# Sorting out graph edges: a threshold on GpSimd for four rows, an edge count in place of tie tests, and one sine for the weights

## The chip, the cores and the metric

The kernel runs on one core of a Trainium2 chip. The metric is the device time of one execution in microseconds (us). The kernel before the change takes 1742.52 us, the median of 4 runs (1740.88 to 1758.24).

## The reference

There are 128 graphs of 64 nodes with 128 features, and a 64x64 matrix of distances for each graph, of which about a quarter is not zero. Four graph layers run one after the other, each as `x = layernorm(x + layer(x, adj))`. The first two are continuous-filter layers, and nearly all work lies in them:

```python
# layer 0 (layer 1 is alike: 64 Gaussians, weight A*A in place of rcut)
f_ij = exp(coeff * (d_ij - offsets)**2)
rcut = 0.5 * (cos(d_ij * pi / 5.0) + 1.0) * (d_ij < 5.0)
y    = x @ w_in2f
W    = (ssp(f_ij @ fw1 + fb1) @ fw2 + fb2) * rcut[..., None]
agg  = einsum('bjf,bijf->bif', y, W)
out  = ssp(agg @ ow1 + ob1) @ ow2 + ob2
```

Layers 2 and 3 are graph convolutions with a normalised adjacency matrix. In layer 0 an edge counts only if its distance is under 5, in layer 1 only if it isn't zero. Since `0.5 (cos(pi d / 5) + 1)` is the square of `sin(pi/2 - pi d / 10)`, the weight of layer 0 can be had from one sine and a square.

## The kernel before

**Slots in place of dense matrices.** The kernel computes filters only for edges that are there. The 64 rows of a graph are put in order of their degree, and eight rows each share a partition group; a row gets as many slots as a fixed table of capacities (CAPS) gives it. For each pair of graphs the slots' distances `d`, column numbers `j` and weights `w` lie in DRAM and are loaded by `loads` two pairs ahead, on the queue of SP. Should the input not fit the assumptions (too many edges in a row, equal distances, and the like), a flag sends the program into a general path at the end; with these inputs it isn't taken.

**The main loop.** Two layers of 64 pairs with three chunks each give 384 iterations. An iteration runs, for a chunk: `filter_in` (TensorE, then Exp and Ln on ScalarE), `gather` (TensorE with a one-hot matrix built on VectorE, then a copy on ScalarE), `filter_out` (TensorE), `message` (VectorE, line 1753, two instructions a chunk), and the sums over slots (VectorE, lines 1777 and 1781). The instructions of TensorE, ScalarE, VectorE, GpSimd and SP stand in the order in which the program issues them (`in_order`), so that each engine works through one fixed queue. Small jobs are Python generators in queues; `run(queue, n)` takes n steps of one. `early` holds the edge search, `side` the spreading of the edges for layer 1, one step an iteration.

**The edge search.** The pairs fall into eight sets of eight (NS = 8). `compact(s)` calls `nearest(s)`, which has the eight rows of a set in a tile `ad` of 128 partitions x 8 rows x 64 columns. It turns distances to negative numbers and absent edges to -1e30 (FAR) and then goes through up to five rounds (ROUNDS): MAX8 finds the eight largest values of a row (into `top`, line 1148), FIND_INDEX8 their columns (`at`, line 1151), and MATCH_REPLACE8 puts -1e30 in their places (line 1155), so that the next round finds the next eight. Tests for equal neighbours and for rows that aren't exhausted follow (lines 1163 to 1172). `pack` copies the found values into dense slots (`dc`, `jc`, on GpSimd except in part of set 0), stores them, and computes the weight `w` with a rounding, an absolute value, a sine on ScalarE, a square, and two masks (lines 1088 to 1098). Set 0 is searched ahead of the loop; sets 1 to 7 are searched inside it, during layer 0. `spread_out` puts between the steps of one set the scatters that prepare the next (`permuted`, `load_x`), one in every PACE steps. The loop takes nine steps of `early` an iteration up to iteration 18, and then PACE on average. After the sets, `late_constants` prepares layers 2 and 3 with further steps.

**Where GpSimd comes in.** Its queue carries the scatters (lines 1008 and 1272, indirect DMAs), the packing copies (1070, 1084), the layernorm's power and scaling (1367, 1372), and the adding of biases (1393, 1624).

## Time and profile before

| | |
|---|---|
| median of 4 runs | 1742.52 us (1740.88 to 1758.24) |
| profiled execution | 1747.6 us, span 1745.8 us, mean granted clock 0.949 |
| PE busy | 1544.4 us (88%), 6812 instructions |
| VectorE (DVE) busy | 1532.6 us (88%), 4485 instructions |
| ScalarE (ACT) busy | 1353.1 us (78%), 1699 instructions |
| GpSimd (POOL) busy | 754.2 us (43%), 1150 instructions |
| MATCH_REPLACE8, line 1155 | 176 instructions, 35.1 us, and as many value loads, 13.8 us |

PE is TensorE's matmuls, PEld its loading of weights, SP the engine that issues most DMAs. The shares are of the whole span; the first 90 us are preparation, layer 0 lasts to about 865 us, and the last 150 us run out with less work. An engine that is 88% busy on average can be full in one stage and wait in another, so the shares must be read by stage.

### The profile page before, as it was taken

To read this page: it belongs to the slowest core of one execution; us is meant where nothing else is said; L and a number is where in the kernel's file an instruction comes from. 1 tells how busy PE (TensorE), PEld (TensorE's weight loads), DVE (VectorE), ACT (ScalarE), POOL (GpSimd) and SP (SyncE) were. 2 spreads that over 40 slices of the span, in tenths; PEclk is the share of its full clock that TensorE was granted. 3 is DMA by queue.
4 is the path that set the end of the run, shared out by engine and by line. 5 is a ranking of instruction groups with operands and counts; after the bars stand their busy time and mean duration, and the time that the engine had idled before them with its cause. 6 is when DMAs were issued, how large, how long until landed. Compare 5 with 4: busy or idle time off the path is not lost.

```text
span 1745.8 us, 24319 instructions
## 1 busy us (share of the span) xinstructions
PE 1544.4 (88%) x6812; PEld 798.0 (46%) x6812; DVE 1532.6 (88%) x4485; ACT 1353.1 (78%) x1699; POOL 754.2 (43%) x1150
## 2 busy tenths in 40 slices
PE   1267799999998989898999999999999999999975
PEld 1123344444444444444544555555555555554444
DVE  6668699999998989889888899999999899998875
ACT  1246678888887878787999988889888888888731
POOL 2354154553646543234411234455443445553434
PEclk9978789999998989899999999999999999999976
DMA  4353354545453544343666655545555454555200
GB/s 148 84 131 93 85 129 115 139 120 132 125 137 94 137 104 121 99 114 94 150 146 147 136 124 119 139 121 140 124 129 128 109 138 114 144 121 134 56 8 21
DMA packets 112658, 202.86 MB, mean 116 GB/s; under 512 B 47214, under 2 KB 63872, under 8 KB 112384
## 3 DMA queue, kind: packets, MB, share of 16 engines
q1 hardware_dynamic: 99856, 185.24, 43.8%
q0 software_dynamic: 8080, 14.47, 2.8%
q10 hardware_dynamic: 4576, 1.49, 0.4%
q8 instruction: 56, 0.92, 0.2%
q14 instruction: 90, 0.74, 0.2%
HBM read 186.66 MB, written 14.45 MB: 115 GB/s over the span
## 4 chain that ended last, share of the span: by engine, by line
PE 34%; DVE 22%; issue 14%; DMA 10%; POOL 10%; ACT 4%; SPq 4%; another core or an unknown queue 1%; ACTq 0%; DVEq 0%; POOLq 0%
PE pw L1725 12%; PE pg L1738 7%; PE px L1712 6%; DMA out_dram<-gz,at_row 6%; DVE m L1753 5%; POOL x_all L1372 3%; DVE agg L1777 3%; SPq L1246 2%; ACT h L936 2%; DVE hot L1697 2%; POOL rs L1367 2%; POOL gz L1372 2%; DVE at L1151 1%; DMA w<-w_dram 1%; PE o L1527 1%
## 5 line engine op out<-in xcount | busy, mean ns | idle before, releaser
L936 ACT ACTIVATE g<-pg 128x672 f32<-128x672 f32 (+12 forms) x384 | 298.9, 778 | 168.4 <-PE pg L1738 124.7
L1738 PE MATMUL pg<-hot,ys 64*128 64x336 f32 (+12 forms) x1536 | 354.8, 540 | 11.8 <-ACT g L936 6.2
L936 ACT ACTIVATE h<-h,half 128x672 f32<-128x672 f32 (+13 forms) x385 | 351.1, 912 | 12.5
L1725 PE MATMUL pw<-h,w_L_gnn_fw 128*128 128x336 f32 (+6 forms) x768 | 287.6, 500 | 48.4 <-DVE m L1753 43.0
L1777 DVE TENSOR_REDUCE agg<-m 128x16 f32<-128x240 f32 (+13 forms) x896 | 325.0, 411 | 2.4
L1725 PE MATMUL pw<-h,w_L_gnn_W2T 128*128 128x420 f32 (+5 forms) x768 | 302.6, 517 | 3.1 <-DVE m L1753 3.0
L1753 DVE SCALAR_TENSOR_TENSOR m<-pw,c_L_gnn_fb,g 128x336 f32<-128x336 f32 (+6 forms) x384 | 202.3, 565 | 41.9 <-PE pw L1725 16.8
L1753 DVE SCALAR_TENSOR_TENSOR m<-pw,c_L_gnn_b,g 128x420 f32<-128x420 f32 (+5 forms) x384 | 225.9, 625 | 10.3 <-PE pw L1725 7.5
L1712 PE MATMUL px<-d,fw 32*128 32x336 f32 (+6 forms) x768 | 171.1, 522 | 49.7 <-ACT d L936 29.7
L936 ACT ACTIVATE h<-px,c_L_gnn_b 128x840 f32<-128x840 f32 (+5 forms) x192 | 176.8, 921 | 45.2 <-PE px L1712 43.3
L1738 PEld LDWEIGHTS pg<-hot,ys 64*128 64x128 f32 x1536 | 119.5, 191 | 197.1 <-ACT h L936 93.5
L1725 PEld LDWEIGHTS pw<-h,w_L_gnn_fw 128*128 128x128 f32 x768 | 140.9, 203 | 148.4 <-DVE m L1753 86.5
L1725 PEld LDWEIGHTS pw<-h,w_L_gnn_W2T 128*128 128x128 f32 x768 | 132.7, 191 | 128.4 <-issue 31.2
L1367 POOL TENSOR_TENSOR rs<-rs,neg_half 128x4 f32<-128x4 f32 x61 | 69.0, 1131 | 274.3 <-DVE rs L1364 272.5
L1697 DVE SCALAR_TENSOR_TENSOR hot<-j,row,w 128x1212 f32<-128x1212 bf16 (+12 forms) x128 | 175.5, 1371 | 11.7 <-DMA w<-w_dram 11.2
L936 ACT ACTIVATE h<-px,c_L_gnn_fb 128x672 f32<-128x672 f32 (+6 forms) x192 | 158.4, 825 | 22.6 <-PE px L1712 9.3
L1712 PE MATMUL px<-d,w1t 64*128 64x420 f32 (+5 forms) x768 | 169.1, 517 | 0.0
L936 ACT ACTIVATE d<-d,neg_off 128x1212 f32<-128x1212 f32 (+12 forms) x128 | 136.3, 1065 | 6.4 <-DMA d<-d_dram 6.4
L1712 PEld LDWEIGHTS px<-d,fw 32*128 32x128 f32 x768 | 60.3, 191 | 147.7 <-issue 66.0
L1008 POOL DMA_INDIRECT rows<-comb,goes x64 | 66.9, 1045 | 131.7 <-DMA rows<-comb,goes 79.7
L1372 POOL TENSOR_SCALAR x_all<-ny,mv,rs 128x128 f32<-128x128 f32 x124 | 110.2, 895 | 3.4
L1008 POOL DMA_INDIRECT out_dram<-gz,at_row x56 | 73.0, 1303 | 53.0 <-DMA out_dram<-gz,at_row 40.0
(255 smaller groups left out, 2282.3 us busy)
## 6 DMA issues: line engine op xcount, KB each, us to landing
d<-d_dram SPq DMA_DIRECT2D x32, 315.0 KB
w<-w_dram SPq DMA_DIRECT2D x32, 315.0 KB
d<-d_dram SPq DMA_DIRECT2D x32, 303.0 KB
w<-w_dram SPq DMA_DIRECT2D x32, 303.0 KB
w<-w_dram SPq DMA_DIRECT2D x32, 252.0 KB
j<-j_dram SPq DMA_DIRECT2D x32, 157.5 KB
j<-j_dram SPq DMA_DIRECT2D x32, 151.5 KB
d<-d_dram SPq DMA_DIRECT2D x16, 300.0 KB
```

What stands on the lines that cost most here:

```text
L936: latest = nc.scalar.activation(out_, in_, func, **kw)
L1008: nc.gpsimd.indirect_dma_start(out=into, out_offset=bass.IndirectOffsetOnAxis(ap=at, axis=0), in_=rows, in_offset=None,)
L1151: nc.vector.max_index(out=at[:, r, cut], in_max=top[:, r, cut], in_values=ad[:, r, 0:A])
L1246: (engine if name == "d" else nc.sync).dma_start(to, dram_ap(slots[layer, name][s], first, [[0, to.shape[0]], [1, n]]))
L1367: nc.gpsimd.tensor_tensor(rstd, rstd, neg_half[:, 0:n], ALU.pow)
L1372: (nc.gpsimd if n == GS else nc.vector).tensor_scalar(dst[:, s, :], y[:, s, :], mv[:, s, 0:1], rstd[:, s : s + 1], ALU.subtract, ALU.mult,)
L1697: nc.vector.scalar_tensor_tensor(hots[n][:, 0:size], j[:, 0:size], near, wt[:, 0:size], ALU.is_equal, ALU.mult)
L1712: nc.tensor.matmul(ps[:, b, 0:n], lhsT=w["w1"][rows, :], rhs=d[rows, col : col + n], start=True, stop=True,)
L1725: nc.tensor.matmul(ps[:, 0 : c["size"]], lhsT=c["w"]["w2"], rhs=c["h"][:, b, :], start=True, stop=True)
L1738: nc.tensor.matmul(ps[:, b, 0:n], lhsT=y[rows, :], rhs=hots[c["n"]][rows, at], start=True, stop=True,)
L1753: nc.vector.scalar_tensor_tensor(messages[n][:, b, at], c["pw"][b][:, 0:size], c["w"]["b2"], c["g"][:, b, :], ALU.add, ALU.mult,)
L1777: nc.vector.tensor_reduce(av[:, :, :, r], both, AX.X, ALU.add)
```

## The change

`take_out`, on GpSimd, replaces MATCH_REPLACE8 for sets 1 to 7: for up to four rows at once it subtracts the smallest of the eight values found from each value, turns "not below" into -1e30, and adds that, writing into a second tile, so that rounds alternate between two tiles. Set 0 keeps MATCH_REPLACE8. The tests for ties become a count: the edges found, with a large penalty for each equal pair, are summed into `found`, and `settle` compares the total with the number of edges counted from the input. In `pack` of layer 0 the copy into `dc` becomes a maximum with -5, so that a missing or far edge lies at the distance where the weight is zero, and the weight is one sine and one square, the square on GpSimd for sets 1 to 7. PACE becomes 3, and the uneven 2, 5, 5 steps of an iteration become an even 3.

```diff
-    PACE = 4
+    PACE = 3
...
-            (nc.vector if layer + s == 0 and r % 2 else nc.gpsimd).tensor_copy(
-                dc[:, to], d[:, r, 0 : caps[r]]
-            )
-            if layer == 0 or r % 2:
+            engine = nc.vector if layer + s == 0 and r % 2 else nc.gpsimd
+            if layer == 0:
+                engine.tensor_scalar(dc[:, to], d[:, r, 0 : caps[r]], -CUTOFF, None, ALU.max)
+            else:
+                engine.tensor_copy(dc[:, to], d[:, r, 0 : caps[r]])
+            if r % 2:
                 yield
...
         if layer == 0:
-            nc.vector.tensor_scalar(w, dc, 1.0 / (2 * CUTOFF), MAGIC, ALU.mult, ALU.add)
-            nc.vector.tensor_scalar(w, w, MAGIC, None, ALU.subtract)
-            yield
-            nc.vector.scalar_tensor_tensor(w, dc, 1.0 / (2 * CUTOFF), w, ALU.mult, ALU.subtract)
-            nc.vector.scalar_tensor_tensor(w, w, -1.0, w, ALU.mult, ALU.max)
-            yield
-            act(w, w, AF.Sin, bias=half_pi, scale=-PI)
-            nc.vector.tensor_mul(w, w, w)
-            yield
-            nc.vector.scalar_tensor_tensor(w, dc, -CUTOFF, w, ALU.is_gt, ALU.mult)
-            nc.vector.scalar_tensor_tensor(w, dc, 0.0, w, ALU.is_lt, ALU.mult)
+            act(w, dc, AF.Sin, bias=half_pi, scale=PI / (2 * CUTOFF))
+            yield
+            (nc.gpsimd if s else nc.vector).tensor_tensor(w, w, w, ALU.mult)
...
+        now, then = av, spare_
+
+        def take_out(rows, k):
+
+            least = top[:, rows, 8 * k + 7 : 8 * k + 8].to_broadcast([P, rows.stop - rows.start, A])
+            nc.gpsimd.tensor_tensor(gone[:, rows], now[:, rows], least, ALU.subtract)
+            nc.gpsimd.tensor_scalar(gone[:, rows], gone[:, rows], 0.0, FAR, ALU.is_ge, ALU.mult)
+            nc.gpsimd.tensor_tensor(then[:, rows], now[:, rows], gone[:, rows], ALU.add)
+
         for k in range(max(ROUNDS)):
...
-            for r in now:
-                nc.vector.max(out=top[:, r, cut], in_=ad[:, r, 0:A])
+            for r in range(n):
+                nc.vector.max(out=top[:, r, cut], in_=now[:, r, :])
+                if s > 0 and r + 1 in (4, more) and r < more:
+                    take_out(slice(0 if r < 4 else 4, r + 1), k)
                 yield
...
-        same = big(f"same{s}", 320).rearrange("p (r k) -> p r k", r=8)
-        nc.vector.tensor_tensor(same[:, :, 0:39], top[:, :, 0:39], top[:, :, 1:40], ALU.is_equal)
-        nc.vector.scalar_tensor_tensor(
-            same[:, :, 0:39], top[:, :, 1:40], FAR / 2, same[:, :, 0:39], ALU.is_gt, ALU.mult
...
-        nc.vector.tensor_reduce(odd[:, 5 + s : 6 + s], same[:, :, 0:40], AX.XY, ALU.add)
-        yield
-        nc.vector.scalar_tensor_tensor(top, top, FAR / 2, top, ALU.is_gt, ALU.mult)
-        yield
-        yield from pack(0, s, top, at)
+        yield from pack(0, s, top, at)
...
+        nc.vector.tensor_scalar(edges, top, FAR / 2, None, ALU.is_gt)
+        yield
+        nc.gpsimd.tensor_tensor(equal[:, :, 1:40], top[:, :, 0:39], top[:, :, 1:40], ALU.subtract)
+        nc.gpsimd.memset(equal[:, :, 0], 1.0)
+        nc.gpsimd.tensor_tensor(top, top, edges, ALU.mult)
         nc.gpsimd.tensor_copy(comb[:, :, 1, :], at)
+        yield
+        nc.gpsimd.tensor_scalar(equal, equal, 0.0, -1000.0, ALU.is_equal, ALU.mult)
+        nc.gpsimd.tensor_scalar(equal, equal, 1.0, None, ALU.add)
+        nc.gpsimd.tensor_tensor(equal, equal, edges, ALU.mult)
+        yield from wait_steps(PACE)
+        nc.vector.tensor_reduce(found[:, s : s + 1], equal, AX.XY, ALU.add)
...
-        run(early, 9 if i < 18 else (PACE - 2, PACE + 1, PACE + 1)[k] if i < 3 * (NP - 8) else 7)
+        run(early, 9 if i < 18 else PACE if i < 3 * (NP - 8) else 7)
```

`settle` gains a reduction of `found`, a reduction of the counted degrees, a difference, and a square that is added to the flag.

## The prediction

> **What bounds the kernel now.** I read the shares of the engines first, then the busy time by stage, then the groups of instructions, then the waits. In the busy time by stage the columns are: window, its length, busy time (and instructions) of each engine, granted clock, DMA share, GB/s.
>
> ```profile
> 90.00:190.00 100.00, 66.71 (x223) 28.61 (x223) 67.19 (x292) 51.81 (x65) 47.58 (x62) 0.76 0.42 103
> 250.00:715.00 465.00, 426.63 (x1869) 210.20 (x1868) 435.56 (x1571) 395.15 (x521) 230.91 (x390) 0.95 0.48 123
> 745.00:865.00 120.00, 114.32 (x548) 60.03 (x546) 107.09 (x272) 103.80 (x142) 49.36 (x51) 0.97 0.49 121
> 1100.00:1600.00 500.00, 495.46 (x2322) 266.36 (x2321) 464.96 (x1076) 432.44 (x512) 236.73 (x248) 1.00 0.53 127
> ```
>
> The order is PE, PEld, DVE, ACT, POOL. From 1100 us (second graph layer) PE is busy 99% of the time, and the change touches nothing there. From 250 to 715 us the edges of five sets are found beside the first layer: DVE 94%, PE 92%, POOL 50%. From 745 us the edges are all found: PE 95%, DVE 89%. So the edge search is felt only before about 745 us. The same windows with the message line alone (two instructions a chunk) give the pace:
>
> ```profile
> 250.00:715.00 465.00, 126.81 (x241) 0.95 0.48 123
> 745.00:865.00 120.00, 34.53 (x69) 0.97 0.49 121
> ```
>
> 465 us over 120.5 chunks is 3.86 us a chunk with the search, 120 over 34.5 is 3.48 without it. The later chunks are smaller: a message there takes 34.53/69 = 500 ns against 126.81/241 = 526 ns, so the fair floor is 3.48 x 1.052 = 3.66 us.
>
> **The change on DVE.** The groups of 250 to 715 us, five sets (the last columns are busy us, mean ns | idle before):
>
> ```profile
> L1151 DVE FIND_INDEX8 at<-comb,ad 128x8 uint16<-128x64 f32 x150 | 30.5, 218 | 0.0
> L1148 DVE MAX8 comb<-ad 128x8 f32<-128x64 f32 x150 | 24.4, 213 | 0.6
> L1155 DVE MATCH_REPLACE8 ad<-comb,ad 128x64 f32<-128x64 f32 x110 | 21.9, 209 | 0.0
> L1155 DVE MATCH_VALUE_LOAD ad<-comb,ad 128x8 f32 x110 | 8.7, 79 | 0.0
> ```
>
> Removed per set of eight pairs, for sets 1 to 7: 22 replacements of 209 + 79 ns = 6.34 us; the tie tests (lines 1163 to 1174 without the reduction) 0.47 + 0.48 + 0.47 + 0.48 = 1.90; of the weights (lines 1088 to 1098) six operations, and the square moves to GpSimd: 0.26 + 0.35 + 0.35 + 0.30 + 0.30 + 0.30 + 0.30 = 2.16. Added: one comparison on 128x320, put between nothing and the 0.42 us of line 1141 on 128x512, taken as 0.3. Net 10.1 us a set, 50.5 us for the five. If DVE alone set the pace, 435.6 - 50.5 = 385.1 us at 94% would last 410 us, 55 less. It does not: PE and the floor of 3.66 us come first, and there DVE would stand at 385.1/120.5 = 3.20 us a chunk, 87%, which is the 89% of the stage without search. So 120.5 x (3.86 - 3.66) = 24 us are won, with ends at 17 (PE's own 426.6 us at its later 95.3%, 448 us) and 46 (no correction for size). Chunks from 190 to 250 us run the same mixture: 3 us more. **Steady search: -27 us (-19 to -58, the far end if DVE alone counts).**
>
> The search keeps its place: a set takes 97 steps of the edge queue now (1 + 30 + 30 + 22 + 2 + 12) at four an iteration, and 72 (1 + 30 + 30 + 6 + 2 + 3) at three, 24 iterations both times. The first 18 iterations stay at nine steps, so the search ends some ten iterations earlier and no load of slots comes later.
>
> **The change on GpSimd.** The nearest rows:
>
> ```profile
> L1372 POOL TENSOR_SCALAR x_all<-ny,mv,rs 128x128 f32<-128x128 f32 x124 | 110.2, 895 | 3.4
> L1570 POOL TENSOR_TENSOR blocks<-a_all,dinv 64x256 f32<-64x256 f32 x60 | 37.4, 623 | 79.8 <-DMA out_dram<-gz,at_row 52.5 <-PE nT L1581 18.7 <-PE px L1712 3.5
> L1393 POOL TENSOR_TENSOR x_all<-x_all,b_L_gnn_ob 128x512 f32<-128x512 f32 x16 | 20.6, 1285 | 61.3 <-PE xT L1388 61.3
> L1177 POOL CAST comb<-at 128x320 f32<-128x320 uint16 x8 | 3.6, 447 | 0.0
> ```
>
> Two-input work on 256 elements is 0.62 us. A tensor_scalar with two immediates isn't in the trace: the cast gives 0.36 us for 256 elements as a lower end, line 1372 (0.9 us for 128, two scalars from memory) scaled gives up to 1.8; I take 1.5, since line 1372 is the same operation. take_out for four rows is then 0.62 + 1.5 + 0.62 = 2.7 us (1.6 with the cast; 4.8 if all three run at some 6.2 ns an element like line 1372). A set has five of four rows and two of one row (about 1.0 us): 16 us (10 to 26). After it come two subtracting or masking operations and one more on 320 elements (0.8 each), two tensor_scalars (0.45 to 1.9 each), a memset and the square of w (0.4): 6.5 us, and 1 us because the eight copies into dc become a maximum. In sum 23 us a set (13 to 36) on top of 230.9/5 = 46 us, in 24 x 3.66 = 88 us: POOL goes from 50% to 78% (68 to 93).
>
> The Trainium skill speaks against this: its page "GPSIMD Engine Reference", section "Engine selection", keeps elementwise work on VectorE, with about twice the time for two inputs, and calls one-input work roughly line rate. The trace shows 0.9 us for 128 elements of one-input work at line 1372, so the second half doesn't hold for that form. By the page's line rate my estimate of take_out would be about 1.5 us, and the forecast some 4 us lower.
>
> **New waits.** DVE is one queue in order. MAX8 of the next round waits for take_out; behind it stand messages, slot sums and one-hots, and PE waits for those to free PSUM. take_out is issued after the fourth MAX8, the next round starts 12 steps later: four iterations, 14.6 us. In these POOL has two take_outs (5.5 us), four scatters of the set ahead and four of the spread set with their 0.3 us gaps (10.4), and about 2 us of layernorm: 17.9 us while both run, eight iterations of 24. It falls some 7 us behind and catches up after; with 2.7 us of its own the take_out still lands inside 14.6. Queued before it can also be a scatter that waits for the one before:
>
> ```profile
> POOL dc L1070 <- DVE comb L1174: 69.7, 5, 20.4
> POOL rows L1008 <- DMA rows<-comb,goes: 54.8, 24, 4.2
> ```
>
> That is up to 4.2 us (total, times, longest). So the margin is thin but there. Two places are tighter. The reduction into found comes four to five steps after its POOL chain is issued, about 6 us, and jc's copies, w and the chain need some 8: 2 us of DVE a set. And Sin now waits for POOL's dc instead of a DVE chain: up to 1 us of ACT, with its table load after it; the stores of d, j and w on the SP queue wait as long, and the slot loads behind them are due only two pairs later. The tiles same and spare_ also hold two of the eight large buffers for a whole set, so that a load of ad on SP's queue may wait for one; I count nothing, since the next ad has some 15 iterations of lead, and leave a wait to the upper end. Seven sets at 2 to 3 us, half of it absorbed by PE's buffers: **+8 us (0 to +35, where each set loses 5).**
>
> DVE and POOL also meet at memory:
>
> ```profile
> L1070 POOL COPY dc<-comb x60: 182/189/1700, 68.5 to 715.5; 128x13 f32<-128x13 f32 x8, 128x14 f32<-128x14 f32 x7, 128x16 f32<-128x16 f32 x6, 128x12 f32<-128x12 f32 x6
> ```
>
> Minimum, median and longest ns: the same small copy mostly takes 189 ns and once 1700. The skill's page "Advanced Engine Details and Errata", section "VectorE Performance Modes", says that the second Vector port is shared with GpSimd and that the two block each other in two-port modes; the outlier fits. Line 1372's mean of 0.9 us already holds such delays, so nothing is added.
>
> **Start-up.** Set 0 stands alone before the loop, from 50 to 72 us, on DVE's path: 1.9 us of tests, 0.5 of masking leave the way ahead of the packing, and 1.9 of weights leave it after; but POOL's tail of 6 us now stands before the scatters of set 1 (from 71.4 us), whose rows DVE needs at 93 us. I count -2 us (-4 to +2). From 90 to 190 us a chunk takes 6.4 us with no engine above 67%; the waits show it:
>
> ```profile
> POOL dc L1070 <- issue: 29.2, 1, 29.2
> ACT g L936 <- remote: 17.5, 2, 9.9
> DVE m L1753 <- remote: 10.0, 2, 7.0
> ```
>
> Engines stand for something outside the profile at 107 to 124 and 165 to 186 us, both times while POOL issues scatters back to back, every 1.28 us, because nothing holds it. take_out would tie POOL to DVE's rounds and thin these bursts; on the other side POOL has some 59 us of work in set 1's eight iterations. **-3 us (-20 to +15).** settle gets five small DVE operations, +1 us at most, beside the messages of the first layer: the flag is read only at the end.
>
> **Sum.** -27 + 8 - 2 - 3 + 1 = -23 us. The profiled execution took 1747.6 us (span 1745.8); 1724.6 in its terms. It lies 5.1 us above the median of 1742.52, so 1719.5 us as a median: 1.3% faster. About 1% is what a measurement of this kernel can tell from no change.
>
> **Rivals.** (1) The waits eat it: found and Sin lose 4 us a set unabsorbed (28 us instead of 8): 1739.5 us, same. For it: POOL at 78%, in order, with scatter waits of 4.2 us. Against it: 14.6 us of lead on the rounds. (2) Slower: POOL becomes the bound of the rounds. If take_out for four rows costs 4.8 us, two of them and the 12.4 us beside them make 22 us where DVE allows 14.6; a set's POOL work is 46 + 36 + 11 (landing waits) = 93 us in 24 iterations, 3.9 us a chunk, so nothing is won in the steady part, the eager first 18 iterations lose 15 us, and found adds 10: 1747.6 + 15 + 10 - 2 + 1 - 5.1 = 1766 us. It decides from about 4.5 us a take_out. For it: line 1372; against it: the two-input rows, 0.62 us. (3) More: DVE sets the pace (-46) and the bursts thin out (-20), waits 5: 1680 us. For it: DVE is the busiest engine at 94%; against it: PE's 92% at a clock of 0.95. That the change computes less than it says I see no sign of: the rounds stay.
>
> **How the numbers follow.** Forecast 0.50 (own range 1700 to 1732), rival 1 0.19, rival 2 0.16, rival 3 0.15. Faster by over 1% (below 1725.1): 0.42 of the forecast's 0.50 and rival 3, 0.57. Slower by over 1% (above 1759.9): most of rival 2, 0.15. The rest, 0.28, is within 1%. The range for 8 in 10 leaves out half of rival 2 and a part of rival 3: 1685 to 1758.
>
> **What would show it.** Right: the group of line 1155 shrinks to 22 for set 0; the DVE share of the search stage falls to about 88% while PE rises to 94 or 95%; chunks at 3.7 us; POOL at 75 to 80%; take_out's tensor_scalar near 1.5 us. Wrong: a large wait of MAX8 or of the found reduction for POOL, POOL above 90% in that stage, or chunks still at 3.86 us.

## The result, and the profile after

No difference: the changed kernel takes 1751.75 us (median), the kernel before 1749.32 us beside it, a ratio of 0.9999 [0.9987, 1.0011] (the brackets hold the 95% interval). Forecast were 1719.5 us, 1.3% faster. The experiments below ran on three chips; on one of them the kernel before takes 1714 us, on the others 1746 and 1749. So times are set side by side only between the two chips that agree; from the third, ratios to the kernel before on that chip are used.

The busy time by stage of the changed kernel, in the columns shown before (window, length, PE, PEld, DVE, ACT, POOL, granted clock, DMA share, GB/s):

```profile
90.00:190.00 100.00, 71.87 (x233) 31.96 (x234) 64.23 (x275) 54.11 (x67) 84.06 (x108) 0.74 0.45 103
250.00:715.00 465.00, 414.01 (x1817) 206.69 (x1814) 387.06 (x1234) 377.93 (x501) 328.91 (x522) 0.94 0.50 121
745.00:865.00 120.00, 114.72 (x552) 59.83 (x550) 108.27 (x267) 107.45 (x148) 43.01 (x33) 1.00 0.48 118
1100.00:1600.00 500.00, 495.48 (x2315) 266.09 (x2314) 466.76 (x1077) 431.95 (x512) 235.75 (x246) 1.00 0.54 127
```

From 250 to 715 us DVE went from 435.6 to 387.1 us, close to the 385.1 that were forecast, though for fewer chunks (below). POOL went from 230.9 to 328.9 us. But PE did not take up the room: 414.0 us, 12 less than before. Of the messages (line 1773, two a chunk) the stretch holds fewer than the 241 of before:

```profile
250.00:715.00 465.00, 123.17 (x234) 0.94 0.50 121
```

The new groups in that stretch, five sets, by form (busy us, mean ns | idle before):

```profile
L1149 POOL TENSOR_SCALAR same<-same 128x256 f32<-128x256 f32 x22 | 26.0, 1181 | 2.0
L1157 DVE MAX8 comb<-ad 128x8 f32<-128x64 f32 x77 | 13.1, 213 | 9.2 <-POOL ad L1150 9.1
L1150 POOL TENSOR_TENSOR zero<-ad,same 128x256 f32<-128x256 f32 x13 | 11.0, 847 | 1.1
L1148 POOL TENSOR_TENSOR same<-zero,comb 128x256 f32<-128x256 f32 x9 | 10.2, 1136 | 0.6 <-DVE comb L1157 0.4
L1148 POOL TENSOR_TENSOR same<-ad,comb 128x256 f32<-128x256 f32 x13 | 9.9, 758 | 23.4 <-issue 16.0 <-DMA d<-d_dram 4.7 <-DVE comb L1157 2.6
L1150 POOL TENSOR_TENSOR ad<-zero,same 128x256 f32<-128x256 f32 x9 | 6.5, 727 | 0.7
```

take_out for four rows is 0.76 + 1.18 + 0.85 = 2.8 us from the first tile to the second and 1.14 + 1.18 + 0.73 = 3.0 us back: the prediction's 2.7 was right.

**Where the gain went.** I took the start of each message and summed the idle time of an engine between the message of chunk 24 and that of chunk 156 (5.5 sets' worth of the search), by the length of the gap. The chunks up to 24 are called the start-up here, those from 24 to 156 the loop.

| kernel | length us | PE busy | PE idle in gaps under 4 us | PE idle in longer gaps | DVE idle |
|---|---|---|---|---|---|
| before | 515.1 | 472.9 | 42.2 | 0 | 36.5 |
| after | 517.4 | 465.9 | 25.4 | 26.1 | 82.4 |

In the ordinary chunks the change wins 16.8 us of idle time and 7.0 us of PE's own busy time, 23.8 in all (the matmuls of the layer are the same; why they were busy 7 us less, no run shows). The forecast was 24 for the 120.5 chunks of five sets. It loses 26.1 us in four long gaps that were not there before. What DVE gave up (44 us) became idle time of DVE (46 us more).

Three of the long gaps (7.2, 4.5 and 9.5 us) stand at the ends of sets, the fourth (4.9 us, at 552 us) in the middle of one. The waits of 250 to 715 us (total, times, longest), lines of the changed kernel:

```profile
POOL rows L1010 <- DMA rows<-comb,goes: 57.0, 27, 4.1
DVE m L1773 <- PE pw L1745: 45.0, 14, 11.7
...
PE px L1732 <- ACT h L938: 26.0, 5, 9.5
...
ACT d L938 <- DMA d<-d_dram: 15.5, 7, 6.1
ACT w L938 <- POOL dc L1075: 15.4, 3, 7.1
```

PE waits five times for ACT's h, once at the end of each of five sets: 7.2, 2.4, 4.5, 9.5 and 2.4 us, 26.0 in all. The first of them, at 296 us, in the timelines of POOL and then of ACT (start, duration, instruction, idle before):

```profile
289.55 1.05 POOL L1010 DMA_INDIRECT rows<-comb,goes  x1 [1.85 <-DMA rows<-comb,goes]
292.10 0.98 POOL L1010 DMA_INDIRECT rows<-comb,goes  x1 [1.51 <-DMA rows<-comb,goes]
294.58 1.32 POOL L1010 DMA_INDIRECT rows<-comb,goes  x1 [1.50 <-DMA rows<-comb,goes]
297.41 1.03 POOL L1010 DMA_INDIRECT rows<-comb,goes  x1 [1.50 <-DMA rows<-comb,goes]
298.51 1.55 POOL L1075 TENSOR_SCALAR dc<-comb 128x30 f32<-128x30 f32 x5
```

```profile
294.22 1.28 ACT L938 ACT_TABLE_LOAD   x1
301.01 0.40 ACT L938 ACTIVATE w<-dc,half_pi 128x132 f32<-128x132 f32 x1 [5.51 <-POOL dc L1075]
301.44 1.28 ACT L935 ACT_TABLE_LOAD   x1
302.73 0.87 ACT L938 ACTIVATE h<-px,c_L_gnn_fb 128x728 f32<-128x728 f32 x1
```

ACT has loaded the table for Sin and stands: POOL's clamped copies (dc) are queued behind four scatters, each of which waits for the landing of the one before. The next h comes at 302.73, PE's next matmul 7.2 us late, DVE's next message (at 308.56) 11.0 us late. Whether this one wait is the cost, or the lateness of POOL behind it, is what the experiments are for.

POOL's lateness reaches the layer in a second way. ACT waits 15.5 us for the slots' distances d, of which the kernel before has nothing in this stretch. The two longest of these waits, 5.7 us at 376 us and 6.1 us at 555 us, lie in the middle of sets, and PE idles 3.8 and 4.9 us behind them: the second is the fourth long gap. The loads of d stand in SP's queue behind a load of spread edges (rows), which waits until the scatters of POOL have landed. SP's own waits for that, 250 to 715 us, in the kernel before and in the changed one:

```profile
SPq L1192 <- DMA rows<-comb,goes: 3.4, 1, 3.4
```

```profile
SPq L1204 <- DMA rows<-comb,goes: 43.3, 6, 13.6
```

### The profile page after: what moved, and what is told of

The parts are those of the page before. It is cut to its first block, busy times and chain, and to the rows that moved or that the text cites. A ratio compares the mean times of both kernels' runs of the same rounds, so it can differ in the third digit from the quotient of the medians.

```text
span 1742.3 us, 24180 instructions
## 1 busy us (share of the span) xinstructions
PE 1536.6 (88%) x6812; PEld 796.4 (46%) x6812; DVE 1482.3 (85%) x4088; ACT 1350.2 (77%) x1699; POOL 911.0 (52%) x1352
## 4 chain that ended last, share of the span: by engine, by line
PE 30%; POOL 22%; issue 15%; DVE 14%; DMA 11%; ACT 5%; SPq 1%; ACTq 0%; DVEq 0%; POOLq 0%
PE pw L1745 10%; PE pg L1758 6%; DMA out_dram<-gz,at_row 6%; PE px L1732 6%; POOL x_all L1392 5%; DVE m L1773 3%; DMA rows<-comb,goes 2%; POOL rs L1387 2%; POOL x_all L1292 2%; POOL perm L1010 2%; ACT h L938 2%; POOL gz L1392 2%; POOL same L1149 2%; DVE agg L1797 2%; POOL rows L1010 1%
## 5 line engine op out<-in xcount | busy, mean ns | idle before, releaser
L1387 POOL TENSOR_TENSOR rs<-rs,neg_half 128x4 f32<-128x4 f32 x61 | 69.2, 1134 | 274.5 <-DVE rs L1384 272.9
L938 ACT ACTIVATE h<-px,c_L_gnn_b 128x840 f32<-128x840 f32 (+5 forms) x192 | 176.8, 921 | 45.1 <-PE px L1732 44.8
L938 ACT ACTIVATE h<-px,c_L_gnn_fb 128x672 f32<-128x672 f32 (+6 forms) x192 | 158.1, 824 | 14.6 <-PE px L1732 5.7
L938 ACT ACTIVATE d<-d,neg_off 128x1212 f32<-128x1212 f32 (+12 forms) x128 | 136.4, 1066 | 21.2 <-DMA d<-d_dram 20.7
L1392 POOL TENSOR_SCALAR x_all<-ny,mv,rs 128x128 f32<-128x128 f32 x124 | 106.3, 864 | 3.5
```

Of the source, the lines that this page charges most:

```text
L938: latest = nc.scalar.activation(out_, in_, func, **kw)
L1387: nc.gpsimd.tensor_tensor(rstd, rstd, neg_half[:, 0:n], ALU.pow)
L1392: (nc.gpsimd if n == GS else nc.vector).tensor_scalar(dst[:, s, :], y[:, s, :], mv[:, s, 0:1], rstd[:, s : s + 1], ALU.subtract, ALU.mult,)
```

## The experiments

### The kernels before and after once more

> The kernel before once more, for stage times on the same chip as the next three runs. Every theory expects what the first profile of it showed, scaled by the chip's clock: chunk 24 of the message loop near 227 us and chunks 24 to 156 in 515 us at a granted clock of 0.95, both some 4% shorter if the chip grants 1.00.

> The changed kernel once more, beside the kernel before on one chip. Every theory expects a ratio of 0.998 to 1.002, chunks 24 to 156 in 0 to 4 us more than before's, and VectorE some 45 to 50 us less busy in that stretch.

Measured: 1745.06 and 1750.08 us, ratio of the changed kernel 1.0027 [1.0006, 1.0049]. Chunk 24 at 224.6 and 224.5 us, then 515.4 and 521.5 us; PE idle in gaps over 4 us 0 and 31.4 us. The accounting above repeats.

### One wait at a time: clamp, scatters, sine

**Clamp on VectorE.** Sin then waits for DVE, not for POOL.

```diff
-                engine.tensor_scalar(dc[:, to], d[:, r, 0 : caps[r]], -CUTOFF, None, ALU.max)
+                nc.vector.tensor_scalar(dc[:, to], d[:, r, 0 : caps[r]], -CUTOFF, None, ALU.max)
```

> The changed kernel, but the eight clamping copies into dc of the first layer run on VectorE for every set, so that the sine no longer waits for GpSimd (VectorE pays 8 x 0.17 us = 1.4 us a set). Theory A (GpSimd's queue runs late, and ScalarE's sine, waiting for dc, passes the delay to all engines: VectorE stood for 11.0, 4.7, 8.2, 11.7 and 4.1 us at the ends of sets 3 to 7): these five gaps shrink below 3 us, 25 to 35 us come back, a ratio near 0.983 to the kernel before. Theory B (TensorE and ScalarE set the pace anyhow and the gaps only replace other waits): the time stays within 0.4% of the changed kernel. Theory C (the late slot loads on SP's queue are what costs): the gaps go but the time falls by less than 8 us, and ScalarE's waits for d stay at 15 us.

Measured: 0.9972 [0.995, 0.9994]; 24 to 156 in 510.6 us. PE's long gaps fall from 26.1 to 6.0 us, but its shorter ones grow from 25.4 to 36.8: of 20 us only 8.6 come back, and 6.8 in time. Theory C comes nearest: less than 8 us, and ACT's waits for d are still 11.6 us.

**Two DRAM tensors for the scatters,** so that one need only wait for the last but one. The slots of the second layer are then partly empty, and both tensors are filled once in the prologue.

```diff
-                rows1[s].rearrange("q a k -> q (a k)"),
+                rows1[s][r % 2].rearrange("q a k -> q (a k)"),
...
```

> The changed kernel, but the spread edges go alternately into two buffers in DRAM, so that a scatter waits for the last but one and not for the one before; the buffers are filled with zeros ahead of the loop, and half of each is read back, so that the edges of the second layer are partly empty (same number of instructions, one DMA more a set). Theory A (GpSimd is late because its queue stands behind chained scatters: 57 us of waits, 27 times, from 250 to 715 us): these waits fall below 15 us, the take-outs of rounds 1 and 2 end some 5 us earlier, the sine waits less, and the time falls by 15 to 25 us in the loop (the fill may give back 3). Rival (GpSimd is late by its added work alone, at 69% busy): the waits go but the lag of the take-outs and the time stay.

Measured: 0.9945 [0.9922, 0.9969]. The fill delays chunk 0 from 88.6 to 97.9 us; 24 to 156 take 499.3 us, 18 less than the changed kernel. POOL's wait in the scatters shrinks to this:

```profile
POOL rows L1010 <- DMA rows<-comb,goes: 12.4, 6, 3.0
```

ACT's waits for d fall from 15.5 to 3.1 us. The gap at the sets' ends stays (20.3 us of PE in gaps over 4 us), and so does Sin's wait for POOL, 14.1 us against 15.4. So of the single parts the chain of scatters cost the loop most, and the two ways are separate: moving the clamp takes away the one, two tensors the other. No run has both. Of the 18 us, 9.4 are busy time of PE, at a granted clock of 0.96 from 250 to 715 us where the changed kernel had 0.94.

**No sine in sets 1 to 7** (the weight is the square of the clamped distance).

```diff
+            if s == 0:
-            act(w, dc, AF.Sin, bias=half_pi, scale=PI / (2 * CUTOFF))
+                act(w, dc, AF.Sin, bias=half_pi, scale=PI / (2 * CUTOFF))
...
-            (nc.gpsimd if s else nc.vector).tensor_tensor(w, w, w, ALU.mult)
+            (nc.gpsimd if s else nc.vector).tensor_tensor(w, dc if s else w, dc if s else w, ALU.mult)
```

> The changed kernel without the Sin of sets 1 to 7: their weights are the square of the clamped distance, by the GpSimd instruction that squared the sine, so the weights differ. ScalarE then neither waits for GpSimd's clamped distances nor changes its table at a set's end. Theory A (GpSimd's lateness reaches the pipeline mainly through ScalarE, which stands behind the Sin): the gaps of VectorE at the ends of sets 3 to 7, 4 to 12 us each, go, chunks 24 to 156 take 25 to 40 us less than the changed kernel's, ratio 0.977 to 0.985. Rival B (the lateness reaches it through the chained scatters, the stores and the slot loads on SyncE's queue): the gaps shrink but the loads stay late, 5 to 12 us less, ratio 0.993 to 0.997.

Measured: 0.9987 [0.9964, 1.001]; 24 to 156 in 513.6 us. Neither theory had this: PE's long gaps stay at 26.6 us although ACT has no Sin to wait for. Another wait for the same late queue, hidden behind Sin's until now, takes its place, at 250 to 715 us:

```profile
DVE found L1190 <- POOL same L1188: 31.7, 5, 10.9
```

(line 1190 here is the changed kernel's 1189). So "found waits for POOL" did not show in the changed kernel's waits only because DVE stood in a message that waited for Sin, and POOL caught up meanwhile. The slot loads stay late, as rival B had it (ACT waits 24.9 us for d), but the gaps do not shrink.

### Both waits together: clamp on VectorE, count later

```diff
         for k in range(max(ROUNDS)):
+            if k == 1:
+                pay()
...
-        nc.vector.tensor_reduce(found[:, s : s + 1], equal, AX.XY, ALU.add)
...
+        owed.append((found[:, s : s + 1], equal))
```

`pay` reduces what is owed, so the count of a set is summed in the second round of the next. The clamp is on VectorE as above.

> The changed kernel with the clamp on VectorE and with the reduction of the count put off into the next set's second round, where its operand has long been there; GpSimd's work of the removal is unchanged. Theory M (one late queue is felt at several points at a set's end, each of which covers the others, so that they must go together): chunks 24 to 156 take 12 to 25 us less than the changed kernel's and the ratio is 0.985 to 0.994. Rival (the waits at a set's end are not what costs; the pace is set by late slot loads behind the chain of scatters): no better than the clamp alone, 0.995 to 0.999.

Measured: 0.9971 [0.9937, 1.0006]; 24 to 156 in 512.6 us; PE idle 44.4 us, 8.9 of it in long gaps. The number is the rival's: taking waits from the consumers, two at once, gets no further than the clamp alone. The rival's reason, late slot loads behind the scatters, fits too: SP waits 54.2 us for them and ACT 16.4 us for d from 250 to 715 us. POOL is as late as in the changed kernel (its waits in the scatters are 62.4 us, and MAX8 waits for it in the start-up as in the changed kernel).

### Parts of the change alone

**The new weights alone, in the kernel before,** with its removal and its tests:

```diff
-            nc.vector.tensor_scalar(w, dc, 1.0 / (2 * CUTOFF), MAGIC, ALU.mult, ALU.add)
...
-            act(w, w, AF.Sin, bias=half_pi, scale=-PI)
...
+            act(w, dc, AF.Sin, bias=half_pi, scale=PI / (2 * CUTOFF))
```

> The kernel before with only the weights of the change: clamp on GpSimd in place of the copy, one sine, the square on GpSimd for sets 1 to 7; the search, the tests and the pace stay. VectorE is relieved of 2.1 us a set. Theory A (the sine's wait for GpSimd costs, but only when GpSimd is late, and here it has half the load): 3 to 8 us faster, waits of the sine for dc under 2 us each. Rival (any wait of the sine for GpSimd costs as much as it saves): unchanged or slower by up to 5 us, with waits of 5 us and more.

Measured: 1.0026 [1.0, 1.0051]; 24 to 156 in 515.6 us. Some 2 us a set less on DVE bring nothing. The time is the rival's, though Sin waits for POOL only once from 250 to 715 us, 3.3 us.

**The new removal alone,** with the tests and weights of before (the lines against the changed kernel):

```diff
-                engine.tensor_scalar(dc[:, to], d[:, r, 0 : caps[r]], -CUTOFF, None, ALU.max)
...
-            act(w, dc, AF.Sin, bias=half_pi, scale=PI / (2 * CUTOFF))
+            nc.vector.tensor_scalar(w, dc, 1.0 / (2 * CUTOFF), MAGIC, ALU.mult, ALU.add)
...
-        nc.vector.tensor_reduce(found[:, s : s + 1], equal, AX.XY, ALU.add)
+        nc.vector.tensor_reduce(odd[:, 5 + s : 6 + s], same[:, :, 0:40], AX.XY, ALU.add)
```

> take_out and the pace of the change alone; the tests for ties, the copies into dc, the weights and their sine (after four operations of VectorE) are those of the kernel before. Theory A (the lag of GpSimd hurts through the sine, and VectorE stands between dc and the sine here, so that it hurts as well): the gaps at the ends of sets stay at 5 us and more, time within 0.4% of the kernel before. Rival (take_out is sound and the parts with GpSimd's count and clamp are what costs): 10 us or more faster than the kernel before.

Measured: 1.0084 [1.0054, 1.0115]: slower. In the loop PE has no gap over 4 us (31.3 us idle in all), but in the start-up MAX8 stands for POOL's take_out. From 90 to 220 us:

```profile
DVE comb L1163 <- POOL ad L1156: 12.1, 4, 5.4
DVE comb L1163 <- POOL zero L1156: 11.2, 4, 4.1
```

Neither theory had this. There is no profile of the kernel before on this chip, so where the 14 us are lost is not shown.

**The removal left out** (all rounds find the same eight edges):

```diff
-                    take_out(slice(0 if r < 4 else 4, r + 1), k)
...
```

> The changed kernel with take_out left out for sets 1 to 7, so that each round finds the same eight values again (the flag ignores the count; the edges are wrong). VectorE does exactly what it does in the changed kernel, GpSimd loses some 15 us a set. Theory A (GpSimd's lag costs the gain): from chunk 24 to 156 it takes 490 us or less, 25 us under the changed kernel, and the sine's gaps on VectorE shrink below 3 us. Theory B (VectorE's relief buys nothing in this loop): within 8 us of 517 us. In the first 18 iterations GpSimd is no longer held, so that the stalls of all engines while it issues scatters back to back return (5 to 10 us later at chunk 24).

Measured: 0.9866 [0.9812, 0.992]; chunk 24 at 195.7 us and then 489.2 us, against 220.5 and 494.9 for the removal alone on the same chip. The start-up came early, against my expectation, and it holds 25 of the 30 us between the two, which differ in the tests and the weights as well. (The chip is the one on which the kernel before takes 1714 us; the ratio isn't to be set beside those of the half-and-half kernels below.)

**The search and the spreading of sets 1 to 7 left out** (their slots hold fixed data), on the same chip:

```diff
-        yield from spread_out(nearest(s), ahead, PACE)
+        yield from spread_out(nearest(s) if s == 0 else wait_steps(72), ahead, PACE)
...
```

> The changed kernel with the search of sets 1 to 7 and the spreading of edges left out (the steps are empty; the scatters that prepare each set and load x stay; the slots are filled ahead of the loop with other distances and one column number, and the flag ignores the count). It shows the floor: what the first layer takes with no search at all. From chunk 24 to chunk 156 the kernel before takes 515.1 us and the changed one 517.4 us. Theory F (the prediction's floor of 3.66 us a chunk): 483 us, PE at 95%. Theory G (the floor lies much higher, so that there was little to win): 500 us or more. Theory H (floor lower, VectorE really sets the pace): 465 us or less.

Measured: 0.9543 [0.9491, 0.9594]. The floor of the first layer:

```profile
250.00:715.00 465.00, 454.99 (x2134) 230.25 (x2133) 403.94 (x980) 419.72 (x571) 142.39 (x130) 1.00 0.48 116
```

132 chunks in 453.1 us, 3.43 a chunk, against the 3.66 the prediction took as the floor. The 453 us are under theory H's 465, but not for its reason: PE is 98% busy here and VectorE 87%. PE's matmul here is 454.99/2134 = 213 ns at a granted clock of 1.00, in the changed kernel 414.01/1817 = 228 ns at 0.94.

### More work for VectorE

**The removal on VectorE,** two operations for four rows:

```diff
-            nc.gpsimd.tensor_tensor(gone[:, rows], now[:, rows], least, ALU.subtract)
...
+            nc.vector.tensor_tensor(gone[:, rows], now[:, rows], least, ALU.is_ge)
+            nc.vector.scalar_tensor_tensor(then[:, rows], gone[:, rows], FAR, now[:, rows], ALU.mult, ALU.add)
```

> The changed kernel with take_out on VectorE, for four rows at once in two operations (comparison, then a multiply-add): five of about 0.75 us and two of 0.35 us, 4.5 us a set, against 6.3 us of the replacements before. GpSimd keeps the clamp, the square and the count. Theory A (GpSimd's lag costs what VectorE gains): MAX8 never waits, GpSimd falls to about 55% in the search stage, the sine's wait halves, and the time is 10 to 20 us below the kernel before. Theory B (the pace is set elsewhere): no change against either kernel.

Measured: 1.0037 [1.001, 1.0064]. The loop gains 5 us (512.2), the start-up loses 13: chunk 24 comes at 238.1 us. GpSimd is busy 55% of 250 to 715 us and MAX8 doesn't wait for it, as theory A had it, but nothing is won. From 90 to 190 us engines stop for something outside the profile, as in the kernel before (22.1 us of ACT's waits are of the kind "remote").

**Clamp and layer norm's scaling on VectorE** (the scaling runs on POOL in four steps of 0.9 us), to free POOL otherwise:

```diff
-            (nc.gpsimd if n == GS else nc.vector).tensor_scalar(
+            (nc.gpsimd if n == GS and not name.startswith("0_") else nc.vector).tensor_scalar(
```

> The changed kernel with the clamp on VectorE, as in the first experiment, and also the four scalings of each layernorm of the first layer on VectorE (eight of 0.37 us a set there, in place of eight of 0.9 us on GpSimd). Theory A (GpSimd's lag is the cost and 7 us less of its work a set shortens it): another 4 to 8 us below the run with the clamp alone, a ratio near 0.993, waits of MAX8 for GpSimd nearly gone. Rival (VectorE's own load is what matters): equal to that run or slower by up to 4 us.

Measured: 1.0644 [1.0596, 1.0693]. The scaling needs POOL's power of the variance, which is still late; now all of DVE's queue stands for it ("DVE x_all L1392 <- POOL rs L1387" 48.2 us, nine times, in the waits of 250 to 715 us). Neither theory had this. Moving an instruction off a late queue while its operand stays there moves the lateness to a queue that matters more.

### Half of the removal on each engine

**Half and half:** the clamp is on VectorE; of a round's rows the first four go out by the threshold on GpSimd, the others by MATCH_REPLACE8 on VectorE (9 of 22 a set, each a step of its own).

```diff
-                if s > 0 and r + 1 in (4, more) and r < more:
-                    take_out(slice(0 if r < 4 else 4, r + 1), k)
+                if s > 0 and r + 1 == min(4, more):
+                    take_out(slice(0, r + 1), k)
...
-            for r in range(more if s == 0 else 0):
+            for r in range(4 if s else 0, more):
                 nc.vector.match_replace(
-                    out=now[:, r, :], ...
+                    out=(then if s else now)[:, r, :], ...
```

> The changed kernel with the clamp on VectorE, and with four of the eight rows of a round taken out by GpSimd's threshold and the other rows by MATCH_REPLACE8 on VectorE (9 of the 22 a set). If GpSimd's lateness is what eats the gain, halving its added work cuts the lag of the removed rows from 11 to 18 us to under 8 us, the start-up (bound by GpSimd in the changed kernel and by VectorE in the one before) ends 5 us or more earlier, and the ratio is 0.985 to 0.993. If the pace of the loop is set by something that neither engine's load touches, the ratio is that of the clamp on VectorE alone, 0.995 to 0.999.

Measured: 1713.42 us, 0.9796 [0.9767, 0.9825], more than either theory had. It beats both kernels:

```profile
250.00:715.00 465.00, 434.92 (x1952) 217.03 (x1950) 419.57 (x1414) 402.84 (x538) 286.58 (x422) 0.97 0.50 123
```

Against the changed kernel on the same chip, chunk 24 is 18.6 us earlier (205.9), and the 132 chunks after it take 492.0 us, 29.5 less, with no gap of PE over 4 us. 11.9 us are given back after chunk 156; the nine more steps a set fit this: settle's count of the edges comes at 779.6 us, long after chunk 156 (697.9), where the changed kernel had it at 747.5 with chunk 156 at 746.0. In sets 3 to 6 the removals of the second round end 2.7 to 12.5 us after the MAX8 they belong to, those of the third 2.6 to 7.5, against 11 to 18 and 4 to 18 in the changed kernel: less late, though not all under the 8 us expected.

**The same without the extra steps:** each replacement in the step of its FIND_INDEX8.

```diff
                 nc.vector.max_index(out=at[:, r, cut], ...)
+                if s > 0 and 4 <= r < more:
+                    nc.vector.match_replace(out=then[:, r, :], ...)
                 yield
```

> The half-and-half kernel (clamp on VectorE, four rows of a round by GpSimd, the rest by MATCH_REPLACE8) with each replacement in the step of its FIND_INDEX8, so that a search has as many steps as in the changed kernel. If the balance of the two engines is what gave 0.9796: ratio 0.975 to 0.985 again, chunk 24 at 203 to 210 us. If the nine more steps, which spread the search thinner, gave it: 0.993 to 0.999.

Measured: 0.983 [0.9758, 0.9902]; chunk 24 at 212.6, then 500.6 us, and settle's count at 714.7 us. The nine steps alone are not the cause: 0.993 to 0.999 lies outside the interval, which takes in the 0.9796. Chunk 24 is later than the 203 to 210 us expected. The removals of the second round still end 7 to 14 us after their MAX8, but from 250 to 715 us no MAX8 waits for them.

**None on GpSimd:** the same for all rows, and no take_out.

```diff
-                if s > 0 and r + 1 in (4, more) and r < more:
-                    take_out(slice(0 if r < 4 else 4, r + 1), k)
...
+                if s > 0 and r < more:
+                    nc.vector.match_replace(out=then[:, r, :], ...)
```

> The changed kernel with the clamp on VectorE and all 22 removals of a set by MATCH_REPLACE8 on VectorE, each in the step of its FIND_INDEX8, so that the number of steps is that of the changed kernel. VectorE has 10 us a set more than in the changed kernel, GpSimd 20 us less. Theory (either engine's overload costs, the best is between): chunk 24 at 215 to 228 us, VectorE 425 to 440 us busy of the 465 between 250 and 715 us, ratio 0.990 to 1.000. If GpSimd's lateness alone costs, and VectorE's load nothing: ratio 0.975 to 0.982, no worse than half and half.

Measured: 0.9979 [0.9942, 1.0016]; chunk 24 at 227.8, then 512.5 us. With the clamp on VectorE and the number of steps unchanged, GpSimd taking out 22 rows a set (the kernel with the clamp moved, on another chip), 13 and 0 gives 0.9972, 0.983 and 0.9979. Both ends are near the kernel before; the middle is 1.7% faster. Of the 12 us of the loop between 13 rows and none, 6.4 are busy time of PE and 5.6 idle time.

The stretch of 250 to 715 us for 13 rows and for none:

```profile
250.00:715.00 465.00, 425.21 (x1890) 212.55 (x1888) 413.36 (x1383) 393.64 (x523) 294.11 (x449) 0.96 0.50 124
```

```profile
250.00:715.00 465.00, 420.07 (x1836) 208.60 (x1836) 415.81 (x1487) 385.49 (x507) 239.47 (x382) 0.94 0.48 121
```

With none, VectorE is busy 415.8 us, less than the 425 to 440 expected, and yet nothing is won.

**Half and half in the start-up alone** (sets 1 and 2; the rest as changed, the clamp on GpSimd):

```diff
-                if s > 0 and r + 1 in (4, more) and r < more:
+                if 0 < s < 3 and r + 1 == min(4, more) or s > 2 and r + 1 in (4, more) and r < more:
...
-            for r in range(more if s == 0 else 0):
+            for r in range((0, 4, 4, 8, 8, 8, 8, 8)[s], more):
```

> The changed kernel with the half-and-half removal (GpSimd four rows of a round, VectorE's MATCH_REPLACE8 the rest) in sets 1 and 2 alone, which are searched in the start-up; sets 3 to 7 as in the changed kernel, the clamp on GpSimd. If the start-up is held by GpSimd in the changed kernel, chunk 24 comes 12 us or more earlier, chunks 24 to 156 take what the changed kernel takes (515 to 523 us), and the ratio is 0.988 to 0.994. If the gain of the half-and-half kernel is the loop's, chunk 24 moves by under 6 us and the ratio is 0.996 to 1.002.

Measured: 0.9912 [0.9882, 0.9942]; chunk 24 at 201.0, then 523.2 us with 34.9 us of PE in long gaps. The start-up's 23 us are independent of the loop, whose long gaps stay.

| kernel | chunk 24 at us | 24 to 156 us | PE idle, of it in gaps over 4 us | granted clock 100 to 225 us |
|---|---|---|---|---|
| before (again) | 224.6 | 515.4 | 44.5, 0 | 0.79 |
| after (again) | 224.5 | 521.5 | 56.1, 31.4 | 0.77 |
| clamp on VectorE (another chip) | 224.1 | 510.6 | 42.8, 6.0 | 0.77 |
| none on GpSimd | 227.8 | 512.5 | 45.1, 0 | 0.81 |
| half, same steps | 212.6 | 500.6 | 39.5, 0 | 0.83 |
| half and half | 205.9 | 492.0 | 32.8, 0 | 0.88 |

## Why the prediction was wrong

**Nearly right: DVE's relief.** 44 us less over the 132 chunks, 7.9 for the 24 chunks of a set, against 10.1 forecast. That the window has 48.5 us less, so close to the 50.5 forecast, is in part luck: it holds 3.5 chunks fewer. The replacements shrank to the 22 of set 0, as named.

**Right in size, in part by luck: what the relief is worth in an ordinary chunk.** -24 us was forecast for the 120.5 chunks of five sets, 23.8 measured in 132 chunks outside the long gaps. The floor from which it was worked out was wrong, though: 3.43 us a chunk where the prediction had 3.66. It corrected the later stage's 3.48 for chunk size and kept that stage's granted clock of 0.97; with no search PE ran at 1.00. (That run leaves out the spreading of edges too, and its chip is the one with the faster kernel before, so the clock need not be all of it.) No kernel here that searches reached either: the half-and-half kernel's 492.0/132 = 3.73 is the nearest of those that compute everything.

**Right: GpSimd's work.** 2.8 to 3.0 us a take_out (2.7 forecast), the tensor_scalar 1.18 us (1.5 forecast, the cast's scaled 0.36 as the lower end), POOL 71% of the stage (78% forecast). The Trainium skill ("GPSIMD Engine Reference", section "Engine selection") calls one-input elementwise work on GpSimd roughly line rate. The trace has the tensor_scalar of one input and two immediates at 1181 ns for 256 elements, no faster than the two-input operations beside it (727 to 1136 ns), so for that form it doesn't hold. (Line 1372, read as 6.2 ns an element for the upper end, is 895/128 = 7.0.)

**Wrong: the term "New waits", +8 us (0 to +35).** Measured in the 132 chunks: +26.1 us in long gaps (31.4 in the second run), 21.2 of them at the ends of three sets and 4.9 behind a late load of slots. That is inside the range of this term, but over three times the size that went into the sum. With 26 in place of 8 the sum gives -5 us, so this term carries 18 of the 23 us by which the forecast missed. Four parts of that step failed.

- "It falls some 7 us behind and catches up after". From the last MAX8 that a take_out reads to the end of its addition, the trace has 2.7 to 6.5 us in the first round of sets 3 to 6, but 11 to 18 us in the second and 4 to 18 in the third. I had counted POOL's work (17.9 us in 14.6) and named the scatters' waits for landing (up to 4.2 us), but had not put them into the 17.9: 27 of them cost 57.0 us in the stage, some 11 us a set, in which nothing behind them starts. The kernel before has nearly as much (54.8 us); new is that take_out stands in the same queue.
- "Up to 1 us of ACT" for Sin. It was 2.7 to 7.1 us where it waited, and the price is ACT's place in the pipeline: 7.2 us of PE and 11.0 of DVE for 5.5 of waiting between two table loads.
- The reduction into found was named in the right place, at 2 us a set. For the first two sets, ahead of chunk 24, it waits 4.8 and 6.3 us; in the loop its wait is hidden by Sin's, and without Sin it is up to 10.9 us. Sin and found are two readers of one late queue; they wait at the same time, so each hides the other. Adding 2 us for the one and 1 us for the other was the wrong sum: at a set's end the lateness of POOL is paid once, whoever stands for it.
- The slot loads were put at nothing ("due only two pairs later", "no load of slots comes later"). ACT waited 15.5 us for them, up to 6.1 at a time, because SP's queue stood 43.3 us for the scatters; with two tensors for the scatters it waited 3.1.

**Start-up: right in size, wrong in mechanism.** -3 us (-20 to +15) was forecast; chunk 24 came 2.8 us earlier. The stops for something outside the profile are gone (no wait of a "remote" kind from 90 to 190 us, where the kernel before had 17.5 us before ACT's g and 10.0 before DVE's messages), but a new wait of MAX8 for take_out took their place, 25.9 us:

```profile
DVE comb L1157 <- POOL ad L1150: 13.1, 5, 6.0
DVE comb L1157 <- POOL zero L1150: 12.8, 4, 4.1
```

POOL is at 84% there. With half of the rows on DVE (same steps) that wait falls to 8.9 us, and in the three kernels with half of the rows there chunk 24 comes 12 to 24 us earlier. So a gain of the size of the prediction's end, -20 us, was within reach where POOL had less to take out. The reason given for it, thinner bursts, is not shown: with no removal at all (on another chip) POOL issues scatters back to back from 94 to 120 and from 131 to 165 us, 0.3 us apart, and no engine stops for something outside the profile.

**The rivals.** The first, "the waits eat it" by Sin and found, was the right one in place, though it left out the slot loads. Its 28 us, for seven sets, lie near the 26.1 to 31.4 measured over five set ends, which is in part luck. It had 0.19. The second, POOL as the bound of the rounds, holds in the start-up alone. Of the signs named for wrong, one came true in the search stage, a chunk took 3.92 us (517.4/132) and not 3.7, and one in the start-up, the wait of MAX8 for POOL.

**What is shown and what is not.** Shown: the gain is in the ordinary chunks and is given back in long gaps, most of it at set ends; taking waits away at the readers brings the time 0.1 to 0.3% under the kernel before, two tensors for the scatters 0.55%, and other waits for the same queue remain; halving the removal on POOL, with the clamp moved, returns 37 us against the changed kernel (1750.08 to 1713.42), 19 of them in the start-up. Not settled: why the loop with no removal on GpSimd is no faster than before's (512.5 against 515.4 us), though no gap is long, DVE idles 53 us of it and PE 45. In its start-up engines stop again for something outside the profile (ACT's waits of the kind "remote", 23.3 us from 90 to 190 us, the half-and-half kernel's 1.4); what that something is, no run shows. Not settled either: why PE's own busy time differs between these kernels, which is half of what the loop gains from none to half, and what the clamp on VectorE and two tensors for the scatters would give together. Nor is it settled how much the extra steps help: 0.9796 and 0.983 overlap.

## What to carry to other kernels

When work is moved to an engine with spare time, sum up its queue in order over one period, with the waits that its DMA-issuing instructions already make, and take the lateness at the point where each reader needs the result, not the busy share: POOL at 71% was up to 18 us late. Look for every reader, also the queue of loads that stands behind a DMA of the late engine. Count the lateness once for readers that wait at the same time, and don't try to mend it at the readers one by one; divide the work so that neither queue is later than its readers can bear, which here turned 0% into 2%. The busy time of the moved instructions, nearly right here, is only half of the sum.

## What the runs showed of the hardware

- An indirect scatter on GpSimd to the tensor that the one before writes waits for that landing: 1.5 to 1.9 us each in the rows shown, with 1.0 to 1.3 us of its own, so 2.5 us a scatter in POOL's queue. With two tensors in turn the waits of a stage fell from 57.0 to 12.4 us.
- Sin between Exp and Ln costs ACT two table loads of 1.28 us each, whether or not it waits: where it did not wait (at 397 us) PE still stood 2.4 us and DVE 4.7.
- PE's granted clock went with its busy share from 250 to 715 us. On one chip: 94% busy, 0.97 and 223 ns a matmul with half and half; 90%, 0.94 and 229 ns with none on GpSimd. With no search, on another chip and with other data, 98%, 1.00 and 213 ns. In the start-up the clock was 0.77 in the changed kernel and 0.88 with half and half. Which of the two drives the other, no run shows.
- GpSimd's operations of one shape vary: in the half-and-half kernel with unchanged steps eight additions of 128x256 averaged 683 ns, four of the other direction 1754 (729 to 2442).
